# Two feed-forward stages of a macaron block: every pass from the ninth tile on queued in a written order

## The chip, the cores and the metric

The kernel runs on one core of one Trainium2 chip, in one launch. The metric is the device time of an execution in microseconds (us): the median of several runs. The engines are TensorE (PE: matmuls and transposes; its weight loads are shown as PEld), VectorE (DVE), ScalarE (ACT), GpSimd (POOL) and SyncE (SP), which issues DMAs.

## The reference

The input x has the shape (2, 2048, 256) in float32, that is 32 tiles of 128 rows. With `ln` the layer norm without weights:

```
x = x + 0.5 * ffn(ln(x))
x = x + attention(ln(x))
x = x + 0.5 * ffn(ln(x))            # the same weights

ffn(x):   h = silu(q4(x) @ q4(w_gate).T) * (q4(x) @ q4(w_up).T)      # 256 -> 704
          return q4(h) @ q4(w_down).T                                # 704 -> 256
q4(x):    blocks of 16 along the last dimension: scale = max(|x|) / 6, at least 1e-12;
          x / scale rounded to 0, 0.5, 1, 1.5, 2, 3, 4, 6 with its sign; times scale
attention: q, k, v complex (256 -> 512 each, with biases);
          scores = (qr kr^T + qi ki^T) / 16, softmax over 2048 keys; out = [wr, wi] @ Wo.T + bo
```

## The kernel before

x stays on chip for the whole execution, in four groups `xs[g]` of eight tiles (GT = 8, NT = 32). The quantised weights are `wgu` (gate and up) and `wd` (down). The kernel has three stages.

**A feed-forward stage** (`ffn`, once with phase 0 and once with phase 1) does this for each tile. Statistics of a group of eight tiles (`Norm`) come from DVE, with one Sqrt on ACT. ACT normalises four tiles into `xl` (L234), and `quant` rounds them: DVE finds the blocks' maxima (L164), scales (L166), takes reciprocals (L168), multiplies (L170), ACT takes absolute values (L179), two DVE passes round (L180, L182), and the last multiplication goes to POOL (L184). TensorE transposes (tx, L403), ACT copies. `product` multiplies by the gate weights and then by the up weights (gu, L428) into one of two PSUM buffers; ACT takes the silu of the first (L442), DVE multiplies by the second (L446). Two tiles' `h` are rounded together with the same `quant`; `turn` transposes h on TensorE (th, L463) and ACT copies (hqT, L464); `back` multiplies by `wd` (po, L472) and DVE adds the result to x (L474).

**The opening** does this for the first eight tiles beside the preparation of the weights. Its work is cut into generators, called threads, that yield after each pass, and `ORDER` lists which thread takes its next step:

```
for name in ORDER.split():
    next(threads[name])
...
fence(begun)
```

`fence` ties each instruction behind the one before it on its engine, so each engine's queue has the order of the list. From the ninth tile on there is no list: the loop over `units` traces the products of a tile, the last projection of an earlier one and the turn of another, and rounds two tiles at a time (one at a time for the last two). The compiler's scheduler sets the order within the engines' queues by its own priorities. While the first stage runs, the loop around it also calls `batches[0].measure` and `batches[0].turned` (statistics, transposes txa and a product `own` for the first batch's attention), and the first attention steps.

**The attention** runs in steps of 1/8 of a group of four query tiles: eight groups, eight steps each, and ten more at the end. A step makes scores (ps, L708) and keeps the running maximum on DVE (`most`, L720); after the eighth, `peak` transposes it (pm, L727) and DVE forms `mx` (L729 to L732), which `highest` turns back (pb, L737). Later steps subtract and take exponentials (L743, L744), sum the weights on POOL (`sums`, L772) and multiply by the values (m, L805). `plain` makes the values' side of one pair of tiles (xn). `residual` adds the constant row `bout`, the bias with what the value bias gives, to four tiles of x on POOL (L848):

```
nc.gpsimd.tensor_tensor(gr.xo, gr.xo, bout.unsqueeze(1).to_broadcast([P, QG, D]), ALU.add)
```

It is traced in the fifth step after the group's scores, but has no tie to anything except readers of x. Phase 1 of `ffn` starts in the last attention steps.

Of the kernel before, what the change touches and what calls it, by code (L numbers as in the profile page):

```python
# [17 lines left out]
P = 128  # L18
BLK = 16
EPS = 1e-5  # L20

# [9 lines left out]

ORDER = """
# [20 lines left out]
def kernel(ctx: ExitStack, tc: tile.TileContext, x, wqT, bq, wkT, bk, wvT, bv, woT, bo,  # L53
# [84 lines left out]
    ones = const.tile([P, P], FP, tag="ones", name="ones")  # L138
    nc.gpsimd.memset(ones, 1.0)
    tiny = const.tile([P, 1], FP, tag="tiny", name="tiny")  # L140
    nc.gpsimd.memset(tiny, 1e-12)
# [15 lines left out]

    def quant(pool, y, n, tag, last, first=None):
# [7 lines left out]
        nc.vector.scalar_tensor_tensor(scale, scale, 1.0 / 6.0, tiny.to_broadcast([P, nb]), ALU.mult, ALU.max)  # L166
        rec = pool.tile([P, nb], FP, tag=f"{tag}_r", name=f"{tag}_r", bufs=2)
        nc.vector.reciprocal(rec, scale)  # L168
        if first is None:
            nc.vector.scalar_tensor_tensor(  # L170
                yb, yb, BELOW, rec.unsqueeze(2).to_broadcast([P, nb, BLK]), ALU.mult, ALU.mult
            )
        else:
            nc.vector.scalar_tensor_tensor(rec, rec, BELOW, ones[:, 0:nb], ALU.mult, ALU.mult)
            first.tensor_tensor(yb, yb, rec.unsqueeze(2).to_broadcast([P, nb, BLK]), ALU.mult)
# [10 lines left out]
    class Norm:  # L186
# [6 lines left out]
        def turns(self, pool):  # L193
# [4 lines left out]

            mv, bn = tile("mv", [P, n, 2]), tile("bn", [P, n, 6])
# [5 lines left out]
            var = tile("var", [P, n])  # L205
            nc.vector.tensor_scalar(var, mv[:, :, 1], EPS, None, ALU.add)
            yield
# [16 lines left out]
            nc.vector.scalar_tensor_tensor(self.shift, mv[:, :, 0], -1.0, rstd, ALU.mult, ALU.mult)  # L224
# [22 lines left out]
    class Rounding:  # L247
# [9 lines left out]
        def turns(self, y, n):  # L257
# [9 lines left out]
            nc.vector.scalar_tensor_tensor(scale, scale, 1.0 / 6.0, tiny.to_broadcast([P, nb]), ALU.mult, ALU.max)  # L267
# [50 lines left out]
    def fold():  # L318
# [63 lines left out]
        nc.gpsimd.tensor_tensor(bb, bq_sb, bk_sb, ALU.mult)  # L382
        ps = weight_bank([P, KE], "wbb")
# [5 lines left out]
    def ffn(phase, store, pools):  # L389
# [19 lines left out]
        def inputs(i0):  # L409
# [10 lines left out]
            yield  # L420
# [28 lines left out]
        def held(i0, n):  # L449
            h = later["pool"].tile([P, n, FF], FP, tag="h", name=f"h{phase}_{i0}", bufs=3 if phase else 4)  # L450
            for u in range(n):
                hs[i0 + u] = h[:, u, :]
            return h.rearrange("p u i -> p (u i)")

        def turn(i):

            hq = hs.pop(i)
            hqTs[i] = later["pool"].tile([P, NR, P], FP, tag="hqT", name=f"hqT{phase}_{i}", bufs=2)
            for r0 in (0, 4):
# [4 lines left out]
                nc.scalar.copy(hqTs[i][:, r0:r0 + len(rs), :], ps[:, 0:len(rs), :])  # L464
                yield

        def back(i):
            g, j = divmod(i, GT)
            hqT = hqTs.pop(i)
            po = p_acc.tile([P, D], FP, tag="acc", name=f"po{phase}_{i}")  # L470
            for r in range(NR):
                nc.tensor.matmul(out=po, lhsT=hqT[:, r, :], rhs=wd[:, r, :], start=(r == 0), stop=(r == NR - 1))  # L472
# [8 lines left out]
        xqTs, hs, hqTs = {}, {}, {}  # L481
        pending, turned = [], []
        first = 0
        if phase == 0:
            first, pending, stats[1] = opening(across, products, held, turn, back)
            yield
        else:
            for i0 in (0, XT):
                for _ in inputs(i0):
                    yield  # L490
            yield

        units = [(i0, HT) for i0 in range(first, NT - HT, HT)] + [(i0, 1) for i0 in range(NT - HT, NT)]
        for i0, n in units:
            if i0 % XT == 0 and i0 + XT < NT and i0 + XT not in xqTs:
                all_of(inputs(i0 + XT))
            h = held(i0, n)
            for u in range(n):
# [3 lines left out]
                if len(pending) > HT:  # L502
                    all_of(turn(pending[0]))
                    turned.append(pending.pop(0))
                yield
            all_of(quant(later["pool"], h, n * FF, "qh", nc.gpsimd if n == HT else nc.vector))
            pending += range(i0, i0 + n)
        while turned:
            following = pending[:1]
            if following:  # L510
                all_of(turn(pending.pop(0)))
            all_of(back(turned.pop()))
            turned += following
            yield

    def opening(across, products, held, turn, back):
# [41 lines left out]
        return 8, list(range(TURNED, 8)), norms["n2"]  # L558
# [39 lines left out]
    class Batch:  # L598
# [3 lines left out]
        def __init__(self, b):  # L602
            self.b = b
            self.xT, self.xn, self.stats = {}, {}, {}

        def measure(self, part):
            g = self.b * tiles // GT + part
            self.stats[g] = normalise(asmall, g, 0, GT)
# [5 lines left out]
        def turned(self, p, kt):  # L614

            if p == 0 and self.b == 0:
                self.rc = asmall.tile([P, tiles], FP, tag="rc", name=f"rc{self.b}")
            nat = kt.tile([P, 2, D], FP, tag="nat", name=f"nat{self.b}_{p}", bufs=2)
            for v in range(2):
                self.norm(nat[:, v, :], 2 * p + v)  # L620
            ps = p_t.tile([P, KD, 2, P], FP, tag="t", name=f"txa{self.b}_{p}")
            for v in range(2):
                for kc in range(KD):
                    nc.tensor.transpose(ps[:, kc, v, :], nat[:, v, ts(kc, P)], ident)  # L624
            self.xT[p] = kt.tile([P, KD, 2, P], FP, tag="xT", name=f"xT{self.b}_{p}", bufs=NP)
            nc.scalar.copy(
                self.xT[p].rearrange("p c v t -> p (c v t)"), ps.rearrange("p c v t -> p (c v t)")
            )
            if self.b == 0:
                for v in range(2):  # L630
                    self.own(nat[:, v, :], 2 * p + v)

# [27 lines left out]
    def attention(batches, at, kt, late):  # L660
# [80 lines left out]
        def weights(gr, s):  # L741
# [5 lines left out]
            if not seven(gr):  # L747
# [3 lines left out]
                else:  # L751
                    for v in range(2):
                        add(gr.sums, gr.sums, both[:, v, :, :], ALU.add)
# [4 lines left out]
        def sums_of_weights(gr, s):  # L758
# [12 lines left out]
            else:  # L771
                add(gr.sums, t[:, 1:3, :], gr.first[:, 1:3, :] if s == 1 else gr.sums, ALU.add)  # L772
# [72 lines left out]
        def residual(gr):  # L845
            g, j = divmod(gr.i * QG, GT)
            gr.xo = xs[g][:, j:j + QG, :]
            nc.gpsimd.tensor_tensor(gr.xo, gr.xo, bout.unsqueeze(1).to_broadcast([P, QG, D]), ALU.add)  # L848
# [160 lines left out]
```

## Time and profile before

| what | us |
|---|---|
| median of 3 runs (lowest to highest) | 1071.6 (1071.26 to 1072.62) |
| the profiled execution | 1072.21 |
| its span, first to last instruction | 1070.4 |
| busy: TensorE matmuls, weight loads | 1047.0, 733.0 |
| busy: DVE, ACT, POOL | 805.9, 470.0, 255.9 |

The mean granted clock of TensorE was 0.998. A line of the profile's groups names the line of the kernel, the engine, the operation and what it writes and reads. A matrix instruction's busy time overlaps that of the next one. In float32 each product of the program appears as two matmul instructions, each transpose as one.

### The profile page before, as it was taken

How to read it: one execution, taken by the hardware profiler on the slowest of the kernel's cores; microseconds unless marked ns; L12 is line 12 of the kernel's file. 1: busy time of each engine (PE TensorE's matmuls, PEld its weight loads, DVE VectorE, ACT ScalarE, POOL GpSimd, SP SyncE). 2: the span in 40 equal slices, each digit the busy share in tenths (PEclk: the TensorE clock that was granted, in tenths of full speed). 3: DMA queues.
4: the chain of work that ended last, by engine and by line, in shares of the span. 5: the costliest groups of instructions: out<-in, count | busy, mean ns of one | idle time of the engine just before them, and what ended most of it. 6: DMA issues, size and time to landing. Idle time of an engine off the chain costs nothing.

```text
span 1070.4 us, 11326 instructions
## 1 busy us (share of the span) xinstructions
PE 1047.0 (98%) x4206; PEld 733.0 (68%) x4206; DVE 805.9 (75%) x1387; ACT 470.0 (44%) x739; POOL 255.9 (24%) x148
## 2 busy tenths in 40 slices
PE   6998999999999999999999999999999999999998
PEld 5676777777765567676675767666655777777776
DVE  7999998867634888576698958678777577777575
ACT  4744644544235635446444533343343244343232
POOL 4564121210103020111124111212481021221110
PEclk9999999999999999999999999999999999999999
DMA  9000000000000000000000000000000000000001
GB/s 320 2 1 1 1 1 1 1 1 1 0 1 1 1 0 1 1 1 1 0 1 1 1 0 1 1 1 1 0 1 1 10 20 10 20 12 19 20 10 40
DMA packets 7286, 13.50 MB, mean 13 GB/s; under 512 B 1344, under 2 KB 3648, under 8 KB 6848
## 3 DMA queue, kind: packets, MB, share of 16 engines
q1 hardware_dynamic: 6128, 12.13, 3.1%
q10 hardware_dynamic: 1104, 0.66, 0.3%
q8 instruction: 33, 0.54, 0.2%
q14 instruction: 21, 0.17, 0.0%
HBM read 8.59 MB, written 4.19 MB: 12 GB/s over the span
## 4 chain that ended last, share of the span: by engine, by line
PE 91%; DVE 5%; ACT 2%; DMA 1%; issue 0%; POOL 0%; ACTq 0%; DVEq 0%; POOLq 0%
PE gu L428 26%; PE ps L708 19%; PE m L805 15%; PE po L472 14%; PE th L463 4%; PE poa L856 3%; PE z L783 3%; PE pu L686 2%; PE tx L403 1%; PE wm L338 1%; PE txa L624 1%; ACT xn L234 1%; DVE h L285 1%; DMA n_gate<-in_w_gate_dram 1%; DVE h L283 1%
## 5 line engine op out<-in xcount | busy, mean ns | idle before, releaser
L428 PE MATMUL gu<-wgu,xqT 128*128 128x352 f32 x1024 | 319.1, 461 | 3.0 <-DVE h L446 2.7
L428 PEld LDWEIGHTS gu<-wgu,xqT 128*128 128x128 f32 x1024 | 188.9, 191 | 98.2 <-DVE h L446 3.8
L708 PE MATMUL ps<-uT,xT 128*128 128x512 f32 x512 | 232.2, 593 | 0.7 <-DVE most L720 0.7
L472 PE MATMUL po<-wd,hqT 128*128 128x256 f32 x768 | 176.1, 379 | 0.0
L472 PEld LDWEIGHTS po<-wd,hqT 128*128 128x128 f32 x768 | 144.7, 190 | 28.2 <-ACT zT L819 0.6
L708 PEld LDWEIGHTS ps<-uT,xT 128*128 128x128 f32 x512 | 95.1, 190 | 93.2 <-issue 81.0
L720 DVE TENSOR_TENSOR most<-ps,most 128x512 f32<-128x512 f32 x112 | 77.0, 687 | 93.5 <-ACT st L715 92.9
L184 POOL TENSOR_TENSOR h<-h,qh_s 128x1408 f32<-128x1408 f32 x26 | 67.5, 2594 | 290.1 <-DVE h L182 248.2
L715 ACT COPY st<-ps 128x512 f32<-128x512 f32 x128 | 74.5, 583 | 134.1 <-PE ps L708 133.6
L805 PE MATMUL m<-tw,xn 128*128 128x256 f32 x448 | 124.9, 380 | 0.0
L464 ACT COPY hqT<-th 128x512 f32<-128x512 f32 (+1 forms) x128 | 55.5, 481 | 156.7 <-PE th L463 154.5
L772 POOL TENSOR_TENSOR sums<-tw,sums 128x512 f32<-128x512 f32 x42 | 56.9, 1354 | 232.2 <-DVE tw L768 212.9
L805 PE MATMUL m<-st,xn 128*128 128x256 f32 x336 | 100.0, 379 | 0.0
L744 ACT ACTIVATE st<-st 128x1024 f32<-128x1024 f32 x64 | 67.4, 1057 | 72.7 <-DVE st L743 72.0
L446 DVE TENSOR_TENSOR h<-h,gu 128x704 f32<-128x704 f32 x64 | 56.3, 879 | 53.3 <-PE gu L428 50.6
L805 PEld LDWEIGHTS m<-tw,xn 128*128 128x128 f32 x448 | 84.8, 190 | 13.1 <-DVE tw L767 1.2
L743 DVE TENSOR_TENSOR st<-st,top 128x1024 f32<-128x1024 f32 x64 | 82.8, 1305 | 0.8 <-ACT top L739 0.8
L805 PEld LDWEIGHTS m<-st,xn 128*128 128x128 f32 x336 | 63.2, 190 | 26.2 <-issue 19.4
L180 DVE SCALAR_TENSOR_TENSOR h<-qh_m,h 128x1408 f32<-128x1408 f32 (+1 forms) x30 | 45.8, 1527 | 33.1 <-ACT qh_m L179 32.9
L442 ACT ACTIVATE h<-gu 128x704 f32<-128x704 f32 x64 | 48.2, 753 | 44.7 <-PE gu L428 44.6
L179 ACT ACTIVATE qh_m<-h 128x1408 f32<-128x1408 f32 (+1 forms) x30 | 38.9, 1297 | 46.1 <-DVE h L170 42.3
L463 PE MATMUL th<-ident,h 128*128 128x128 f32 x384 | 53.1, 273 | 1.4 <-ACT hqT L464 1.4
(175 smaller groups left out, 1266.6 us busy)
## 6 DMA issues: line engine op xcount, KB each, us to landing
out_dram<-x SPq DMA_DIRECT2D x15, 256.0 KB, 2.1
x<-in_x_dram SPq DMA_DIRECT2D x3, 1024.0 KB, 13.0
n_down<-in_w_down_dram SPq DMA_DIRECT2D x1, 704.0 KB, 9.4
n_up<-in_w_up_dram SPq DMA_DIRECT2D x1, 640.0 KB, 6.0
x<-in_x_dram ACTq DMA_DIRECT2D x1, 512.0 KB, 5.3
wq_sb<-in_wqT_dram SPq DMA_DIRECT2D x1, 512.0 KB, 7.0
wk_sb<-in_wkT_dram SPq DMA_DIRECT2D x1, 512.0 KB, 4.7
wv_sb<-in_wvT_dram SPq DMA_DIRECT2D x1, 512.0 KB, 6.6
```

Source lines behind the costliest of these rows:

```text
L184: last.tensor_tensor(yb, yb, scale.unsqueeze(2).to_broadcast([P, nb, BLK]), ALU.mult)
L428: nc.tensor.matmul(out=ps[:, b2, 0:HALF], lhsT=xqT[:, i % XT, kc, :], rhs=wgu[:, kc, ts(which * 2 + b2, HALF)], start=(kc == 0), stop=(kc ...
L446: nc.vector.tensor_tensor(h, h, up, ALU.mult)
L463: nc.tensor.transpose(ps[:, r - r0, :], hq[:, chunk(r)], ident)
L472: nc.tensor.matmul(out=po, lhsT=hqT[:, r, :], rhs=wd[:, r, :], start=(r == 0), stop=(r == NR - 1))
L708: scored = nc.tensor.matmul(out=ps, lhsT=gr.of.xT[s][:, c, v, :], rhs=gr.uT[:, c, :], start=(c == 0), stop=(c == KD - 1),)
L715: nc.scalar.copy(piece[:, v, :], ps)
L720: seen = nc.vector.tensor_tensor(gr.most, ps, gr.most, ALU.max)
L743: nc.vector.tensor_tensor(piece, piece, gr.top.unsqueeze(1).to_broadcast([P, 2, Q]), ALU.subtract)
L744: nc.scalar.activation(piece, piece, AF.Exp, scale=SCALE)
L772: add(gr.sums, t[:, 1:3, :], gr.first[:, 1:3, :] if s == 1 else gr.sums, ALU.add)
L805: i = nc.tensor.matmul(out=gr.m[k], lhsT=left, rhs=right, start=first, stop=last)
```

## The change

- **Both feed-forward stages from the ninth tile on are threads.** `woven` makes a thread for every group's statistics (`n`), four input tiles (`x`), pair of `h` to be rounded (`h`), tile's products (`p`), turn (`t`) and last projection (`b`); in the first stage also the attention's statistics (`m`), batch 0's transposes (`a`) and its first six steps (`q`). `FFN0_ORDER` (492 steps) and `FFN1_ORDER` (422) list which one goes on, and `fence` ties each engine's queue to that order. A new generator `rounding` yields after each pass. The second stage keeps the loop for its first eight tiles, with the input tiles traced earlier.
- **All transposes of this part are TensorE's**; `turn` writes into a pool of its own with three buffers (`hqT2`).
- **The last two tiles of the second stage go in halves** of 352 columns (`halves`), each with products, silu, multiplication and rounding on DVE.
- **The bias** is queued on POOL behind the group's latest sum of weights. The values' side of batch 1 (`plain`) leaves one step out after half of its pairs.
- The lower bound of the scales and two factors become immediate constants in place of constant tensors (`tiny`, `ones`); `Norm` forms the negative mean (`least`) earlier.

```diff
+FFN0_ORDER = """
+t4 n2 n2 x12 t5 x12 n2 p9 n2 p8 m0 p9 x12 n2 p8 t4 n2 x12 n2 n2 x12 p9 n2 n2 n3 p8 x12 x12 b4 p8 x12
+n2 t6 p9 h8 h8 n3 t5 x12 x12 x12 p11 p11 h8 p10 x12 n2 n3 n2 p11 p10 t6 p11 n3 n2 h8 n2 x12 h8 p10
...
+p31 b25 p30 b25 h28 a7 h28 t26 a7 q a7 p31 t26 h28 h28 q a7 b24 t27 h30 b24 q h30 h30 b26 t29 b26
+h30 h30 b27 t28 t29 b27 h30 h30 q a5 h30 b29 a5 b29 a5 t28 b28 t30 b28 t31 a5 q t30 a7 t31 b31 b30
+b31 a5 a7 b30
+"""
+FFN1_ORDER = """
+h6 n3 n2 h6 b3 p8 h6 p8 n3 h6 p8 p9 n2 n2 n2 h6 p8 n2 n2 p9 t4 p9 h6 t4 h6 t5 p10 t5 p9 n2 p11 n2
+p10 h8 n2 h8 h8 n2 p10 h6 n2 t6 n2 n2 p11 n3 n2 n2 n2 h8 t6 n3 b3 x16 x16 b4 h8 x16 t7 p10 h8 x16 b4
...
+p28 h28 h26 t25 h28 t25 h30a b23 t26 h28 t26 h28 h30a h30b b23 b24 h28 h30b h28 h30a t27 h30b h31b
+h30a b25 t27 h30a b24 h28 b26 h30b h28 h31a h30a h30a h31b b26 t29 h30b h30a h30b h31b b25 h31a h31b
+h31b h30b t28 h30b h30b h31b b27 t29 h31b h31a h31b t28 b27 t30 h31a h31a b28 h31a b28 h31b h31a
+h31a t30 h31a b29 b29 t31 t31 b30 b30 b31 b31
+"""
...
+    def rounding(pool, tag, y):
+        n = y.shape[1]
...
         yb = y.rearrange("p (b k) -> p b k", k=BLK)
         scale = pool.tile([P, nb], FP, tag=f"{tag}_s", name=f"{tag}_s", bufs=2)
         nc.vector.tensor_reduce(scale, yb, AX.X, ALU.max, apply_absolute_value=True)
         yield
-        nc.vector.scalar_tensor_tensor(scale, scale, 1.0 / 6.0, tiny.to_broadcast([P, nb]), ALU.mult, ALU.max)
+        nc.vector.tensor_scalar(scale, scale, 1.0 / 6.0, TINY, ALU.mult, ALU.max)
+        yield
         rec = pool.tile([P, nb], FP, tag=f"{tag}_r", name=f"{tag}_r", bufs=2)
+        nc.vector.reciprocal(rec, scale)
+        yield
+        nc.vector.scalar_tensor_tensor(
+            yb, yb, BELOW, rec.unsqueeze(2).to_broadcast([P, nb, BLK]), ALU.mult, ALU.mult
+        )
+        yield
+        m = pool.tile([P, n], FP, tag=f"{tag}_m", name=f"{tag}_m", bufs=1)
+        nc.scalar.activation(m, y, AF.Abs, scale=STEPS)
+        yield
+        nc.vector.scalar_tensor_tensor(y, m, LEAST, y, ALU.max, ALU.add)
+        yield
+        nc.vector.scalar_tensor_tensor(y, m, LEAST, y, ALU.max, ALU.subtract, reverse1=True)
+        yield
+        nc.gpsimd.tensor_tensor(yb, yb, scale.unsqueeze(2).to_broadcast([P, nb, BLK]), ALU.mult)
+        yield
...
+        rec = pool.tile([P, nb], FP, tag=f"{tag}_r", name=f"{tag}_r", bufs=2)
+        nc.vector.tensor_scalar(scale, scale, 1.0 / 6.0, TINY, ALU.mult, ALU.max)
...
-            nc.vector.scalar_tensor_tensor(rec, rec, BELOW, ones[:, 0:nb], ALU.mult, ALU.mult)
+            nc.vector.tensor_scalar(rec, rec, BELOW, None, ALU.mult)
...
         def held(i0, n):
-            h = later["pool"].tile([P, n, FF], FP, tag="h", name=f"h{phase}_{i0}", bufs=3 if phase else 4)
+            pool, bufs = (later["pool"], 4 - phase) if phase or i0 else (wpool, 1)
+            h = pool.tile([P, n, FF], FP, tag="h", name=f"h{phase}_{i0}", bufs=bufs)
             for u in range(n):
                 hs[i0 + u] = h[:, u, :]
-            return h.rearrange("p u i -> p (u i)")
+            wholes[i0] = h.rearrange("p u i -> p (u i)")
+            return wholes[i0]

         def turn(i):

+            if i in hqTs:
+                return
             hq = hs.pop(i)
-            hqTs[i] = later["pool"].tile([P, NR, P], FP, tag="hqT", name=f"hqT{phase}_{i}", bufs=2)
+            pool, tag = place()
+            hqTs[i] = [(r, wd[:, r, :]) for r in range(NR)], pool.tile([P, NR, P], FP, tag=tag, name=f"hqT{phase}_{i}", bufs=3 if tag == "hqT2" else 2)
+            hqT = hqTs[i][1]
             for r0 in (0, 4):
                 ps = p_t.tile([P, 4, P], FP, tag="t", name=f"th{phase}_{i}_{r0}")
                 rs = range(r0, min(r0 + 4, NR))
                 for r in rs:
                     nc.tensor.transpose(ps[:, r - r0, :], hq[:, chunk(r)], ident)
-                nc.scalar.copy(hqTs[i][:, r0:r0 + len(rs), :], ps[:, 0:len(rs), :])
+                nc.scalar.copy(hqT[:, r0:r0 + len(rs), :], ps[:, 0:len(rs), :])
                 yield
+        def place():
+            if "turned" in later:
+                return later["turned"], "hqT2"
+            return (later["pool"] if phase else wpool), "hqT"

...
-            hqT = hqTs.pop(i)
+            chunks, hqT = hqTs.pop(i)
             po = p_acc.tile([P, D], FP, tag="acc", name=f"po{phase}_{i}")
-            for r in range(NR):
-                nc.tensor.matmul(out=po, lhsT=hqT[:, r, :], rhs=wd[:, r, :], start=(r == 0), stop=(r == NR - 1))
+            for k, (r, right) in enumerate(chunks):
...
-        xqTs, hs, hqTs = {}, {}, {}
+        def woven(order, pending, more):
+            begun = len(nc.cur_bb.bb.instructions)
+            single = NT - HT if store else NT
+            def tile_products(i):
+                if i not in hs:
+                    held(i - i % HT, HT)
+                yield from products(i)
+            def inputs_of(i0):
+                g, j0 = divmod(i0, GT)
+                xl = xp.tile([P, XT, D], FP, tag="xl", name=f"xl{phase}_{i0}")
+                for u in range(XT):
+                    normed(xl[:, u, :], g, j0 + u, stats[g])
+                    yield
+                yield from rounding(xp, "qx", xl.rearrange("p u d -> p (u d)"))
+                for u in range(0, XT, 2):
+                    across(i0, xl[:, u:u + 2, :], u, 2)
+                    yield
+            def pair_of(i0):
+                yield from rounding(later["pool"], "qh", wholes[i0])
+            def halves(i, b2):
+                if i not in hs:
+                    held(i, 1)
+                h = hs[i][:, ts(b2, HALF)]
+                gu = []
+                for which in range(2):
+                    gu.append(p_big.tile([P, 2, 512], FP, tag="big", name=f"gu{phase}_{i}_{b2}{which}")[:, 0, 0:HALF])
+                    for kc in range(KD):
+                        nc.tensor.matmul(
+                            out=gu[which],
+                            lhsT=xqTs[i - i % XT][:, i % XT, kc, :],
+                            rhs=wgu[:, kc, ts(which * 2 + b2, HALF)],
+                            start=(kc == 0),
+                            stop=(kc == KD - 1),
+                        )
+                    yield
+                    if which == 0:
+                        nc.scalar.activation(h, gu[0], AF.Silu)
+                        yield
+                nc.vector.tensor_tensor(h, h, gu[1], ALU.mult)
+                yield
+                yield from quant(later["pool"], h, HALF, "qh", nc.vector)
+                yield
+            threads = dict(more)
+            for i0 in range(GT + XT * (1 + phase), NT, XT):
+                threads[f"x{i0}"] = inputs_of(i0)
+            for g in range(2, NG):
+                stats[g] = Norm(g, 0, GT)
+                threads[f"n{g}"] = stats[g].turns(small)
+            for i0 in sorted(i for i in hs if i not in pending and i % HT == 0) + list(range(GT, single, HT)):
+                threads[f"h{i0}"] = pair_of(i0)
+            for i in range(single, NT):
+                for b2 in range(2):
+                    threads[f"h{i}" + "ab"[b2]] = halves(i, b2)
+            for i in range(pending[0], NT):
+                threads[f"t{i}"] = turn(i)
+            for i in range(GT, single):
+                threads[f"p{i}"] = tile_products(i)
+            for i in range(pending[0], NT):
+                threads[f"b{i}"] = back(i)
+            for name in order.split():
+                next(threads[name])
+            for name, thread in threads.items():
+                assert next(thread, None) is None and next(thread, threads) is threads, name
+            fence(begun)
...
+        xqTs, hs, hqTs, wholes = {}, {}, {}, {}
+        if phase == 0:
+            pending, stats[1] = opening(across, products, held, turn, back)
+            yield
+            woven(FFN0_ORDER, pending, later["more"])
+            return
...
+        for i0 in range(0, GT, HT):
+            h = held(i0, HT)
+            coming = inputs(i0 + XT + HT) if i0 % XT == XT - HT else None
...
+                if coming and u == 0:
+                    while next(coming) != "rounded":
+                        pass
+                elif coming:
+                    all_of(coming)
                 yield
-            all_of(quant(later["pool"], h, n * FF, "qh", nc.gpsimd if n == HT else nc.vector))
-            pending += range(i0, i0 + n)
-        while turned:
-            following = pending[:1]
-            if following:
-                all_of(turn(pending.pop(0)))
-            all_of(back(turned.pop()))
-            turned += following
-            yield
+            if i0 + HT < GT:
+                all_of(quant(later["pool"], h, HT * FF, "qh", nc.gpsimd))
+                pending += range(i0, i0 + HT)
+        woven(FFN1_ORDER, pending, {f"b{i}": back(i) for i in turned})
...
         def measure(self, part):
             g = self.b * tiles // GT + part
-            self.stats[g] = normalise(asmall, g, 0, GT)
+            self.stats[g] = Norm(g, 0, GT)
+            return self.stats[g].turns(asmall)
...
             else:
-                add(gr.sums, t[:, 1:3, :], gr.first[:, 1:3, :] if s == 1 else gr.sums, ALU.add)
+                gr.summed = add(gr.sums, t[:, 1:3, :], gr.first[:, 1:3, :] if s == 1 else gr.sums, ALU.add)
                 gr.first = None
...
         def residual(gr):
             g, j = divmod(gr.i * QG, GT)
             gr.xo = xs[g][:, j:j + QG, :]
-            nc.gpsimd.tensor_tensor(gr.xo, gr.xo, bout.unsqueeze(1).to_broadcast([P, QG, D]), ALU.add)
+            with tc.issue_after(gr.summed.ins):
+                nc.gpsimd.tensor_tensor(gr.xo, gr.xo, bout.unsqueeze(1).to_broadcast([P, QG, D]), ALU.add)
...
+    ffn0_pools[1]["turned"] = ffn0.enter_context(tc.tile_pool(name="f0_t", bufs=1, side="right"))
...
-    begun = 0
-    done = 0
-    for n, _ in enumerate(stage, GT - 2):
-        if n >= tiles + 4 and begun < NP:
-            if begun % (GT // 2) == 0:
-                batches[0].measure(begun // (GT // 2))
-            batches[0].turned(begun, kt)
-            begun += 1
-        if n >= NT - 2:
+    done = 6
+    def scored():
+        for _ in range(done):
             next(att)
-            done += 1
+            yield
+    more = {f"m{part}": batches[0].measure(part) for part in range(tiles // GT)}
+    more.update({f"a{p}": batches[0].turned(p, kt) for p in range(NP)})
+    more["q"] = scored()
+    ffn0_pools[1]["more"] = more
+    all_of(stage)
     ffn0.close()
-    late["pool"] = ctx.enter_context(tc.tile_pool(name="late", bufs=1, side="right"))
+    late_stack = ctx.enter_context(ExitStack())
+    late["pool"] = late_stack.enter_context(tc.tile_pool(name="late", bufs=1, side="right"))
     per = tiles // QG * NP
-    plain = [(done + p, 0, p) for p in range(NP)] + [(per + LAG + p + 1, 1, p) for p in range(NP)]
+    plain = [(done + p, 0, p) for p in range(NP)] + [(per + LAG + p + 1 + (p >= NP // 2), 1, p) for p in range(NP)]
...
-    for _ in stage:
-        pass
+    late_stack.close()
+    hp["turned"] = ctx.enter_context(tc.tile_pool(name="f1_t", bufs=1, side="right"))
+    all_of(stage)
```

## The prediction

> **What bounds the kernel now.** I read the page's busy shares and slices first, then the waits of TensorE, then the stretches around the change, then single instructions in the timeline.
>
> ```profile
> PE 1047.0 (98%) x4206; PEld 733.0 (68%) x4206; DVE 805.9 (75%) x1387; ACT 470.0 (44%) x739; POOL 255.9 (24%) x148
> ...
> PE   6998999999999999999999999999999999999998
> ...
> DVE  7999998867634888576698958678777577777575
> ```
>
> TensorE is busy all the time, so nothing shortens the kernel except less matmul work or fewer gaps on TensorE. DVE is nearly full in the slices up to about 215 us and has room later.
>
> "Busy" overstates TensorE, since its instructions overlap; what counts is the distance from start to start:
>
> ```profile
> 89.38 7.26 PE L428 MATMUL gu<-wgu,xqT 128*128 128x352 f32 x24
> ```
>
> 24 of them take 7.26 us with the last one's 0.46, so 6.80 / 23 = 0.2955 us each, though one lasts 0.46. In the same way, from other rows of the timeline: 0.2155 us for 256 columns, 0.109 for a transpose, 0.429 for 512 columns.
>
> The replaced first stretch runs from tile 8's first product (89.1 us) to the end of the sixth attention step (339.6). It holds 384 gate and up matmuls (113.5 us), 336 of the last projection (72.4), 240 transposes (168 th, 40 tx, 32 txa: 26.2), 48 score matmuls (20.6) and 32 of the queries (6.9): 239.6 us of work in 250.5 us. So 10.9 us are gaps or a slow clock. Where:
>
> ```profile
> 89.10:98.60 9.50, 7.54 (x27) 4.59 (x25) 9.47 (x15) 2.74 (x5) 2.59 (x1) 1.00 0.00 1
> 98.60:104.50 5.90, 5.26 (x17) 3.14 (x18) 5.73 (x19) 0.83 (x2) 1.93 (x1) 0.71 0.00 0
> 104.50:126.70 22.20, 20.41 (x94) 15.31 (x92) 21.25 (x46) 14.02 (x23) 4.52 (x2) 1.00 0.00 1
> 126.70:215.00 88.30, 87.59 (x380) 64.58 (x381) 79.42 (x127) 44.72 (x69) 18.87 (x8) 1.00 0.00 1
> 89.10:339.60 250.50, 244.69 (x1043) 175.64 (x1041) 187.98 (x302) 115.69 (x193) 47.94 (x20) 0.99 0.00 1
> ...
> 580.00:588.00 8.00, 5.70 (x22) 3.01 (x21) 7.79 (x14) 2.27 (x4) 3.85 (x3) 1.00 0.00 0
> ...
> 850.00:1067.00 217.00, 216.40 (x959) 162.69 (x957) 155.63 (x181) 79.69 (x129) 38.81 (x16) 1.00 0.05 18
> ```
>
> (Columns: stretch, length, busy us of PE, PEld, DVE, ACT and POOL, granted clock, DMA.) Where PE has gaps, DVE has none: 9.47 of 9.50, 5.73 of 5.90. After the first gap the clock was 0.71 over 5.9 us, which costs 0.29 x 5.9 = 1.7 us. The waits of TensorE from 89 to 340 us name the two causes:
>
> ```profile
> PE gu L428 <- DVE h L446: 2.7, 2, 2.0
> PE tx L403 <- POOL xl L184: 2.4, 2, 1.8
> ```
>
> A product waits until DVE has emptied a PSUM bank; transposes wait for a rounded input. In both, DVE was doing something less urgent.
>
> **The change part by part.** *TensorE's work:* turns, products, last projections and the six `q` steps are the same matmuls, and transposes were on TensorE already. So 0 us, and what can be won is gaps alone.
>
> *First stage in one given order.* I summed the passes that FFN0_ORDER lists, with durations of this trace (DVE: pair passes of 128x1408 1.61 each, reciprocal 0.69, scale 0.25, multiplication 0.88, addition 0.415; input passes of 128x1024 1.22; statistics 0.41; POOL 2.61 and 1.94). The whole order holds 239.5 us of TensorE, 196 of DVE, 120 of ACT and 41 of POOL. Running sums: when TensorE has 75.6 us behind it, DVE has 70.8; at 150.8, 139.7; at the end DVE is 43 behind. So DVE fills 94% of the first 75 us and 76% of the rest. Next I took the TensorE work ahead of each consumer, minus the DVE work (and POOL pass) ahead of its producer. All are positive if DVE never waits; the narrowest are p11's bank (3.0 us), x12's transposes (3.7), p15's bank (3.9), t15 (4.9); from x24 on all exceed 8. DVE enters late: its last pass of the opening ends at 92.8, TensorE starts tile 8 at about 89.2, so 3.6 us. That makes p11 wait some 0.6 us, and the others have little left for ACT's part of a rounding.
>
> How much is left as gaps? Lower end: 0.6. Upper end: the opening, the one part that already runs in a given order, lost 2.6 us between 27 and 89 us with DVE at 98%, or 4.2%; over 250 us that is 10.5. The new order resembles it only in its first 75 us: 4.2% of 75 = 3.2. I add 0.5 for the rest and 0.9 for half a chance of one more slow-clock stretch of 1.7. I take 4.6 us, against 10.9 now: **saved 6.3**.
>
> [...] Here a gap of 2.04 us was followed by 0.71, while one of 1.85 us at 126.75 was followed by 1.00. [...]
>
> *Statistics, batch 0's transposes and query steps* are now threads: each `a` still issues two ACT passes, four transposes, a copy and two DVE products; each `n` or `m` one Sqrt with its table loads (1.28 us each). They are in the sums above. ACT has half of its time free, which hides them; a silu behind a Sqrt could be some 2.8 us late, inside the leads except in the first 75 us.
>
> *Bias added later.* Before, the eight POOL additions of 128x1024 went wherever their readers were done, four at 331 to 342 us, one at the worst place:
>
> ```profile
> 334.43 2.33 DVE L697 TENSOR_SCALAR rcg<-rc,bqbk 128x4 f32<-128x4 f32 x1
> ...
> 584.82 2.39 POOL L848 TENSOR_TENSOR x<-x,bout 128x1024 f32<-128x1024 f32 x1
> ...
> 585.64 1.58 DVE L731 TENSOR_TENSOR mx<-mx,rcg 128x4 f32<-128x4 f32 x1
> ...
> 587.57 0.62 PE L737 MATMUL pb<-ident,mx 128*128 128x128 f32 x4 [1.58 <-DVE mx L732]
> ```
>
> A four-element DVE pass, 0.15 to 0.22 us otherwise, took 1.58 and 2.33 beside POOL's 2.4 us, and TensorE waited. Gaps around these: 1.2 us at 339 to 344, and 0.89 + 1.75 = 2.6 at 581.9 and 587.6. Now each addition is queued on POOL behind a sum of weights in step 4 of its group; the maximum's chain runs in step 7 and later, some 20 us away. Behind it on POOL stand the next group's or steps' sums, whose readers (the freeing of `tw`, then the values) have a step of about 7 us. Additions at 555.6, 572.0 and 599.3 delayed no matmul, so moved ones cost 0, or 2.4 if that cover fails. The `plain` of batch 1 also skips step 39, whose DVE was full (7.79 of 8.00). Saved between 0 and 3.8; I take 0.8 + 2.0 = **2.8**, since other passes remain there.
>
> *Second stage.* From 850 us there is 214.6 us of matmul work in 217.0 with the last one's end, about 2 us of gaps. DVE enters with no arrears; sums in its order: 49.9 of DVE at 56.4 of TensorE, 167.6 at 210.3. Narrowest leads 2.6 and 3.3 us, from x24 on over 14. Best 0.7 left, worst 4.2% of 217 = 9.1. I take 1.5: **saved 0.5**.
>
> *Tiles 30 and 31 in halves.* A DVE pass of 128x704 is 0.89, of 128x1408 1.62, so each cut adds 0.16; twelve cut passes (1.9 us) and four times half a scale and reciprocal more (1.3) add some 3 us of DVE, where it has 35 us of lead. The last store follows the last addition as before: 0. *Scale without a constant tensor, the new `least`, a third `hqT`:* below 0.1 us each on DVE, hidden by the same leads; 0 in the first stage too, where one more 0.16 pass would cost at most itself.
>
> [...] Beside POOL, DVE passes of two SBUF tensors got longer (128x128: 1.32 instead of 0.28). The order has 17 POOL passes in the first stage. From its DVE work between each and the next two-tensor pass I get an estimate of 11 us blocked in all, 3.5 of it in the first 75 us. [...]
>
> [...]
>
> **Sum.** 6.3 + 2.8 + 0.5 = 9.6 us. From the profiled execution's 1072.2 (span 1070.4): 1062.6. The median of the runs, 1071.6, is 0.6 lower, so 1062.0.
>
> **The rivals.** [...]
>
> *B. Fixed orders stall at the head of queues, slower:* in a strict order nothing can pass a late pass, and TensorE stalls at the opening's 4.2% everywhere. The first stage then keeps 10.5 us (saves 0.4), the second has 9.1 (costs 7.1), attention still saves 2.8: 1071.6 + 3.9 = 1075.5. It decides once the second stage has over 5.2 us of gaps (2 now) while the first saves only 0.4. For it: only 2 us can be won from 850 us on, 7 lost. Against: leads above 13 us there.
>
> *C. Evened out:* the first stage has 7 us of gaps (saves 3.9), the second 6 (costs 4.0), and attention saves nothing: 1071.7.
>
> *D. The bias does not move* where TensorE waits, or something else fills its place: 2.8 missing: 1064.8.
>
> **How the numbers follow.** The measurement tells about 0.2%, 2.1 us, from no change. Forecast 0.46, A 0.14, D 0.08: together faster, 0.68. C: 0.08. B: 0.24. Lowest bound: all gaps but 0.6 and 0.7 gone and 3.8 in attention, 10.3 + 3.8 + 1.3 = 15.4, 1056.2. The range leaves out that extreme and B's end: 1057.0 to 1074.5; the forecast with A and D alone would be 1057 to 1067.
>
> **What would show it.** Right: the first stage with its six score steps ends near 333 us instead of 339.6; the two waits above fall under 1 us each; no x<-x,bout at 331 to 342 or 585; DVE's share in the first 75 us above 95%. Wrong: new waits of gu on h or tx on xl after 180 us, th on hqT, a clock below 1.00 after 110 us, or more than 4 us of gaps from 850 us on.

## The result and the profile after

The changed kernel takes 1058.5 us, the kernel before 1071.8 beside it: a ratio of 0.9875 (95% interval 0.9858 to 0.9892), or 13.4 us less. The forecast was 1062.0 (1057.0 to 1074.5). The profiled execution took 1058.3 with a span of 1056.5.

The same parts of the page of the changed kernel:

```profile
PE 1040.6 (98%) x4206; PEld 732.0 (69%) x4206; DVE 808.1 (76%) x1408; ACT 470.0 (44%) x742; POOL 259.3 (25%) x148
...
PE   6999999999999999999999999999999999999998
...
DVE  7998998896764987566778967676868569878875
```

TensorE has the same 4206 matmuls and the same 98%; DVE is 2 us busier. Nothing here shows a gain, since the engines did nearly the same work in a shorter span. The stretches that begin at the ninth tile show it. They are cut at the places of the earlier table, and the columns are the same (length, busy us of PE, PEld, DVE, ACT, POOL, clock, DMA):

```profile
89.20:98.70 9.50, 9.50 (x38) 6.28 (x36) 8.44 (x27) 6.31 (x11) 2.59 (x1) 1.00 0.00 1
98.70:104.60 5.90, 5.90 (x29) 4.59 (x28) 5.41 (x9) 2.19 (x4) 0.00 (x0) 1.00 0.00 0
104.60:126.80 22.20, 22.20 (x101) 16.74 (x100) 21.04 (x31) 9.48 (x15) 4.52 (x2) 1.00 0.00 1
...
89.20:329.30 240.10, 239.86 (x1037) 175.05 (x1035) 187.84 (x298) 110.79 (x179) 43.39 (x18) 1.00 0.00 1
```

TensorE is busy 9.50 of 9.50, 5.90 of 5.90, 22.20 of 22.20, at full clock, and DVE has a little idle time where it had none. The first stage with its six score steps now needs 240 us for 239.6 us of matmuls. All waits of TensorE between 89 and 850 us (total, times, longest):

```profile
PE tx L471 <- ACT hqT L538: 0.6, 1, 0.6
PE po L552 <- DVE most L876: 0.2, 1, 0.2
```

None is left after 850 us. For the account I summed, over each stretch, the distances from one matmul's start to the next less the usual distance of its size (gaps and slow clock together):

| stretch (ended by) | before | after |
|---|---|---|
| first matmul's start, and the opening | 8.3 + 8.9 | 8.0 + 8.5 |
| first stage from tile 8 to the 48th score matmul | 10.4 | 1.2 |
| attention, to its last score matmul | 5.4 | 2.3 |
| rest of attention, second stage's tiles 0 to 7 | 0.4 | 1.3 |
| second stage from tile 8 | 2.1 | 0.4 |

The rows differ by 13.8 us in all, the spans by 13.9. Some 0.7 lies before the changed part and varies from run to run: its first product starts at 89.48 us in this profile and at 90.12 when the changed kernel ran again (`changed_again`). One row got worse.

### The profile page after: what moved, and what is told of

The parts are those of the page before. It is cut to its first block, busy times and chain, and to the rows that moved or that the text cites. A ratio compares the mean times of both kernels' runs of the same rounds, so it can differ in the third digit from the quotient of the medians.

```text
span 1056.5 us, 11296 instructions
## 1 busy us (share of the span) xinstructions
PE 1040.6 (98%) x4206; PEld 732.0 (69%) x4206; DVE 808.1 (76%) x1408; ACT 470.0 (44%) x742; POOL 259.3 (25%) x148
## 4 chain that ended last, share of the span: by engine, by line
PE 93%; DVE 4%; DMA 1%; ACT 0%; issue 0%; SPq 0%; DVEq 0%; ACTq 0%
PE gu L496 27%; PE ps L864 20%; PE po L552 16%; PE m L961 15%; PE th L537 4%; PE poa L1013 3%; PE z L939 3%; PE pu L842 3%; PE tx L471 1%; PE gu L595 1%; DMA wq_sb<-in_wqT_dram 1%; PE txa L777 1%; DMA n_up<-in_w_up_dram 1%; DVE bn L267 0%; PE pm L883 0%
## 5 line engine op out<-in xcount | busy, mean ns | idle before, releaser
L496 PE MATMUL gu<-wgu,xqT 128*128 128x352 f32 x992 | 307.5, 460 | 0.9 <-DVE sd L281 0.5
L496 PEld LDWEIGHTS gu<-wgu,xqT 128*128 128x128 f32 x992 | 183.5, 190 | 92.8 <-issue 2.6
L220 POOL TENSOR_TENSOR h<-h,qh_s 128x1408 f32<-128x1408 f32 x24 | 63.6, 2649 | 265.4 <-DVE h L218 237.6
L538 ACT COPY hqT<-th 128x512 f32<-128x512 f32 (+1 forms) x128 | 58.4, 479 | 155.6 <-PE th L537 152.9
L961 PEld LDWEIGHTS m<-tw,xn 128*128 128x128 f32 x448 | 84.8, 190 | 13.4 <-DVE tw L923 1.0
L537 PEld LDWEIGHTS th<-ident,h 128*128 128x128 f32 x384 | 47.3, 141 | 17.4 <-issue 8.0
L537 PE MATMUL th<-ident,h 128*128 128x128 f32 x384 | 57.0, 273 | 0.3 <-ACT hqT L538 0.3
L216 DVE SCALAR_TENSOR_TENSOR h<-qh_m,h 128x1408 f32<-128x1408 f32 x24 | 41.5, 1731 | 19.1 <-ACT qh_m L213 19.0
```

What stands on the lines that cost most here:

```text
L220: nc.gpsimd.tensor_tensor(yb, yb, scale.unsqueeze(2).to_broadcast([P, nb, BLK]), ALU.mult)
L496: nc.tensor.matmul(out=ps[:, b2, 0:HALF], lhsT=xqT[:, i % XT, kc, :], rhs=wgu[:, kc, ts(which * 2 + b2, HALF)], start=(kc == 0), stop=(kc ...
L537: nc.tensor.transpose(ps[:, r - r0, :], hq[:, chunk(r)], ident)
L538: nc.scalar.copy(hqT[:, r0:r0 + len(rs), :], ps[:, 0:len(rs), :])
L961: i = nc.tensor.matmul(out=gr.m[k], lhsT=left, rhs=right, start=first, stop=last)
```

## The experiments

Each kernel below was timed beside the kernel before, which had medians of 1071.6 to 1072.0 on those chips. The changed kernel itself took 1058.5 us the first time and 1058.9 the second, so half a microsecond between two medians shows little; where less than 1 us is at stake, the gaps in the traces decide.

**One stage at a time.** `first_alone` leaves `woven` to phase 0; phase 1 runs by the old loop:

```diff
+        units = [(i0, HT) for i0 in range(first, NT - HT, HT)] + [(i0, 1) for i0 in range(NT - HT, NT)]
+        for i0, n in units:
...
-        woven(FFN1_ORDER, pending, {f"b{i}": back(i) for i in turned})
...
```

> The changed kernel, but the second stage runs by the old loop over units (tiles of the second stage not in a written order, last tiles whole); first stage in its order, bias tied, batch 1's values shifted. Theory (gaps are filled where each part is, and the parts add): the second stage's 2 us of gaps come back, so 1058.5 + 2 = 1060.5 us, with TensorE's gaps before 830 us as in the changed kernel. Rival (the second stage's order won more than its own gaps, for instance by letting attention's end overlap): 1063 or more.

Measured: 1059.2 us. The second stage's gaps came back (2.1 us from its tile 8 on, 0.7 of them its old wait of `th`), but 0.9 us of gaps ahead of it went. So the second stage's part of the change is worth 0.8 us, by the medians and by these gaps alike, less than its own gaps.

`second_alone` does the reverse, with `woven(FFN0_ORDER, ...)` replaced by the old loop and the old calls around it.

> The changed kernel, but the first stage from the ninth tile on runs by the old loop; the second stage's order, the tied bias and batch 1's shift stay. Theory: the first stage's gaps, some 10 us, come back: 1058.5 + 10 = 1068.5 us, with waits of gu on h and of tx on xl near 99, 103 and 127 us and a clock below 1 after the first. Rival (the first stage's gain came from the tie of the bias at 331 to 342 us): about 1062.

Measured: 1067.6 us, so the first stage's order is worth 9.1 us. The waits came back at their places. TensorE from 89 to 850 us in this run, and the stretch with the slow clock:

```profile
PE gu L496 <- DVE h L514: 2.8, 2, 2.0
PE tx L471 <- POOL xl L249: 2.2, 2, 1.7
```

```profile
98.60:104.50 5.90, 5.34 (x18) 3.11 (x18) 5.74 (x18) 0.82 (x3) 1.93 (x1) 0.71 0.00 0
```

The bias is tied in this kernel, so the rival, that the tie won the first stage's time, falls. The third `hqT`, the immediate constants and the new `Norm` are in this kernel too, and its row for the first stage is 10.1 us, against 10.4 in the kernel before; so these smaller edits win at most 0.3 us there.

**What in the order does it.** `no_tie` traces the same lists but drops one line:

```diff
             for name, thread in threads.items():
                 assert next(thread, None) is None and next(thread, threads) is threads, name
-            fence(begun)
```

> The changed kernel with both written orders kept as the order in which the program is traced, but without the fence, so that nothing ties an instruction to the one before it on its engine and the compiler's scheduler may reorder. Theory (the fixed order in each queue is what fills the gaps): several us of gaps come back in the two stages, 1062 to 1068 us. Rival (tracing the passes in this sequence is enough, the scheduler keeps nearly this order): within 1 us of 1058.5.

Measured: 1067.2 us; 8.7 us of the 13.4 are gone. The sequence in the program is not enough; the ties hold each queue to it. (Whether another written order, tied, would do as well was not tried.) From 89 us to the end TensorE's three longest waits were for other things than in the old loop:

```profile
PE po L552 <- ACT hqT L538: 2.9, 1, 2.9
PE gu L496 <- ACT h L510: 1.6, 1, 1.6
PE th L537 <- ACT xT L779: 1.3, 1, 1.3
```

All three ended with ACT. At 99.27 us a product waited for a silu that stood behind the loading of a table (1.28 us) after a Sqrt.

**How close the first stage runs.** `late_3us` and `late_10us` put 8 and 24 needless DVE passes ahead of the order:

```diff
 FFN0_ORDER = """
+z z z z z z z z 
 t4 n2 n2 x12 t5 x12 n2 p9 n2 p8 m0 p9 x12 n2 p8 t4 n2 x12 n2 n2 x12 p9 n2 n2 n3 p8 x12 x12 b4 p8 x12
...
+            def extra():
+                bn = small.tile([P, 6], FP, tag="zz", name=f"zz{phase}", bufs=1)
+                for _ in range(8):
+                    nc.vector.bn_stats(bn, xs[0][:, 0, :])
+                    yield
...
```

> The changed kernel with eight needless statistics passes (0.41 us each, 3.3 us of DVE in all) ahead of all DVE passes of the first stage's order. In the changed kernel the input x12 is ready 0.7 us before its transposes and p9's bank is free 0.2 us before p11 needs it. Theory (DVE has no slack in the first 15 us of the order, and TensorE takes the delay over less these margins): gaps of 2.5 to 3.2 us in TensorE near 102 to 113 us, 1061 to 1061.5 us, more by up to 1.7 if the clock falls. Rival (DVE's 43 us of slack over the stage absorbs it): within 0.7 us of 1058.5.

> The same with 24 needless passes, 9.8 us of DVE. Theory: TensorE loses 9 to 9.7 us in the first 25 us of the order and nothing later, and the clock falls to half once or twice (1.7 us each): 1067.5 to 1071.5. Rival (slack absorbs most): under 1063.

Measured: 1059.5 and 1068.1 us. The passes held DVE longer than expected: each starts 0.46 us after the one before it, so the first statistics behind them begin 3.6 and 11.0 us late. TensorE waited once in each run. The waits of the one and then of the other:

```profile
PE tx L472 <- POOL xl L221: 1.2, 1, 1.2
```

```profile
PE gu L497 <- DVE h L515: 7.1, 1, 7.1
```

In start-to-start distances these are 1.3 and 7.3 us, so some 2.2 and 3.7 us were absorbed. Both expectations fail: TensorE did not take the whole delay, and 43 us of slack did not swallow it. Part of it went into DVE's own waits for ACT and TensorE, which are gone in both runs (0.96 us at 95.0 and 0.35 at 99.0 in the changed kernel). The rest is the margin of the consumer that came late first. That is x12's transposes in the one run, with the 0.7 us of the expectation. In the other it is p11's first product, and the expectation has its margin wrong. In `late_3us` this product starts while p9's multiplication has not begun:

```profile
102.32 7.27 PE L497 MATMUL gu<-wgu,xqT 128*128 128x352 f32 x24
...
103.33 0.83 DVE L515 TENSOR_TENSOR h<-h,gu 128x704 f32<-128x704 f32 x1
```

So it needs only the multiplication before that one, p8's, which in the changed kernel ended at 100.26 us for a start at 102.42: 2.2 us to spare, not 0.2. Nothing later in the order was late in either run. The second run lost about 2.4 us more to a halved clock (0.80 on average from 101 to 118 us). So the order starts with 2 to 4 us to spare on DVE, by consumer; beyond that nearly the whole delay reaches TensorE.

**The bias.** `bias_alone` puts two edits into the kernel before:

```diff
...
-            nc.gpsimd.tensor_tensor(gr.xo, gr.xo, bout.unsqueeze(1).to_broadcast([P, QG, D]), ALU.add)
+            with tc.issue_after(gr.summed.ins):
+                nc.gpsimd.tensor_tensor(gr.xo, gr.xo, bout.unsqueeze(1).to_broadcast([P, QG, D]), ALU.add)
...
-    plain = [(done + p, 0, p) for p in range(NP)] + [(per + LAG + p + 1, 1, p) for p in range(NP)]
+    plain = [(done + p, 0, p) for p in range(NP)] + [(per + LAG + p + 1 + (p >= NP // 2), 1, p) for p in range(NP)]
```

> The kernel before with two edits alone: the bias queued behind the sum of weights, and batch 1's values one step later from its fifth pair on. Theory (POOL's addition holds up DVE's small passes before TensorE's wait): the gaps of 1.2 us at 339 to 344 and 2.6 us at 582 to 588 go, 1071.8 - 3 = 1069 us. Rival (something else becomes late in the same place): 1071 to 1072.

Measured: 1068.3 us, 3.5 us faster. The additions moved to 381, 437, 498, 560 us and so on (in the changed kernel they start between 371.6 and 774.0, none near 331 to 342 or 585). The waits of `pb` and `pm` are gone and no others came in their place, so that rival falls.

`both_free` takes the same two edits out of the changed kernel, `plain_old` only the shift of `plain`, `bias_free` only the tie.

> The changed kernel with the bias not tied to the sums and batch 1's values at their old steps. Theory: the attention's two places lose again what they lost before, 1.2 + 2.6 us, less where the first stage's order has moved the steps: 1058.5 + 3 = 1061.5. Rival (with the attention's first steps moved into the first stage, the bias finds harmless places by itself): within 0.5 us of 1058.5.

> The changed kernel with the values' side of batch 1 at its old steps; the bias stays queued behind the sums. The kernel without either lost 10.2 us: 7.4 of gaps at 341 to 345 and 348.7 with a halved clock, 2.6 at 579 and 585. Theory (POOL's bias addition is what blocks DVE, the shift adds little): at most 1 us lost, 1058.5 to 1059.5. Rival (step 39 is too full for DVE even without the bias): the 2.6 us at 570 to 575 come back, 1061.

> The changed kernel with only the tie of the bias taken away; batch 1's shift stays. The kernel with neither took 1068.7, and the shift alone taken away cost 0.2. Theory (the tie carries both places): 1068 to 1069, with additions at 331 to 348 us and TensorE waiting for mx and most beside them, and at 580 to 588 again. Rival (the shift alone would have mended the place at 579 to 585): 1066, with the first place's gaps only.

Measured: 1068.7, 1058.7 and 1068.4 us; the changed kernel took 1058.9 when it ran beside `bias_free`. So the shift is worth at most 0.2 us, and the tie 9.5 us here, against 3.5 for both in the old kernel. My expectation for `both_free` (1061.5) was wrong by 7 us: the parts do not add. POOL's, DVE's and TensorE's rows of `bias_free` show why (start, us, engine, line, what):

```profile
335.26 4.91 POOL L1004 TENSOR_TENSOR x<-x,bout 128x1024 f32<-128x1024 f32 x2 [0.57 <-ACT xn L300]
```

```profile
335.32 2.45 DVE L811 TENSOR_TENSOR xn<-xn 128x128 f32<-128x128 f32 x1
...
337.90 2.42 DVE L813 TENSOR_TENSOR xn<-xn 128x128 f32<-128x128 f32 x1
...
341.31 3.32 PE L864 MATMUL ps<-uT,xT 128*128 128x512 f32 x4 [3.86 <-DVE most L876]
...
348.52 0.62 PE L893 MATMUL pb<-ident,mx 128*128 128x128 f32 x4 [1.39 <-DVE mx L888]
```

Two additions in a row hold POOL for 4.91 us. Two small DVE passes of about 0.28 us take 2.45 and 2.42 beside them. The running maximum stands behind those, and the next scores wait 3.86 us for their PSUM bank. In the old kernel the sixth score step ended at 339.6 us, so these passes of `plain`, which follow it, began at 341, when the additions (331 to 342) were nearly over:

```profile
339.93 2.35 POOL L848 TENSOR_TENSOR x<-x,bout 128x1024 f32<-128x1024 f32 x1 [0.67 <-ACT xn L234]
```

```profile
340.96 1.47 DVE L655 TENSOR_TENSOR xn<-xn 128x128 f32<-128x128 f32 x1
...
342.36 0.28 DVE L656 TENSOR_TENSOR xn<-xn 128x128 f32<-128x128 f32 x1
```

The new order has six steps done by 324 us, `plain` comes 6 us earlier, and it meets the additions, which did not move. Of the 9.7 us of gaps that the attention has more than in the changed kernel, 7.5 lie here and 2.3 at the second place (579 to 585 us). And the gap costs clock:

```profile
335.00:355.00 20.00, 14.75 (x39) 7.02 (x38) 15.02 (x22) 10.91 (x19) 7.17 (x3) 0.91 0.00 0
```

A clock of 0.91 over 20 us is 1.8 us more. The same stretch of the changed kernel has TensorE busy 19.97 of 20.00 and POOL idle:

```profile
335.00:355.00 20.00, 19.97 (x68) 11.69 (x69) 15.86 (x49) 13.92 (x23) 0.00 (x0) 1.00 0.00 0
```

**Halves.** `whole_tiles` gives the steps of the first halves to whole tiles:

```diff
+            def whole(i, b2):
+                if b2 == 1:
+                    for _ in range(9):
+                        yield
+                    return
...
+                yield from products(i)
+                yield from quant(later["pool"], hs[i], FF, "qh", nc.vector)
+                yield
...
-                    threads[f"h{i}" + "ab"[b2]] = halves(i, b2)
+                    threads[f"h{i}" + "ab"[b2]] = whole(i, b2)
```

> The changed kernel with tiles 30 and 31 of the second stage as wholes: the products, silu, multiplication and rounding of a tile all stand where the first half's steps stand in the order. Theory (DVE leads by over 30 us there, so the halves bring nothing): within 0.3 us of the changed kernel. Rival (halves shorten the end): 0.5 to 1 us slower, with a gap in TensorE before the last turns.

Measured: 1060.2 us, the changed kernel beside it 1058.9: 1.3 us slower, the rival and somewhat more. TensorE waits before one of the last turns:

```profile
1047.97 0.89 DVE L249 TENSOR_TENSOR h<-h,qh_s 128x704 f32<-128x704 f32 x1
...
1049.01 0.85 PE L537 MATMUL th<-ident,h 128*128 128x128 f32 x6 [1.34 <-DVE h L249]
```

Neither the kernel before nor `first_alone`, whose old loops round the same two tiles whole, has this wait. So it belongs to whole tiles at these places of this order; an order rewritten for whole tiles was not tried. From tile 8 of the second stage on, `whole_tiles` has 1.9 us of gaps, the old loop 2.1 and the changed kernel 0.4: nearly all that the second stage's order won, it won with the halves.

**A version meant to be faster.** The worse row of the account is a gap of 0.77 us at 837.8, where the transposes of x12 follow the six of a turn directly. `tx_earlier` moves them ahead of the last projection:

```diff
                 all_of(products(i0 + u))
+                if coming and u == 1:
+                    all_of(coming)
                 if turned:
                     all_of(back(turned.pop()))
...
-                elif coming:
-                    all_of(coming)
                 yield
```

> The changed kernel with the transposes of x8 and x12 in the second stage's first eight tiles moved ahead of the same step's last projection and turn. In the changed kernel TensorE waits 0.77 us at 837.8, where these transposes stand right behind six others and both PSUM buffers still wait for ACT's copies. Theory: that gap goes and nothing takes its place, since 2.6 us of projection now lies between the two groups of transposes: 0.8 us less than the changed kernel on the same chip, about 1057.7. Rival (the copies are then late for the turn behind): no change within 0.2.

> The changed kernel once more, beside its variants on the same chip: 1058.5, as before, with 0.3 either way.

Measured: 1058.0 us (1057.8 to 1058.7, four runs) and 1058.9 (1058.6 to 1059.0). The medians differ as I expected, but the trace does not bear it out. The gap only moved to the next user of those PSUM banks, 0.68 us instead of 0.77:

```profile
838.39 3.72 PE L1013 MATMUL poa<-wvo,zT 128*128 128x256 f32 x16 [0.51 <-ACT hqT L538]
```

From tile 8 of the first stage on, the two profiled runs' gaps differ by 0.1 us; the rest of the 0.9 lies in the first 90 us, which the edit does not touch. So the rival holds: the next step behind the turn waits instead. That this version is faster is not shown.

## Why the prediction was right, and where its sizes were off

**TensorE bound by gaps alone** held: the same work, start to start, to the us, and every lost us found as a gap or a slow clock.

**First stage: 6.3 us expected, 9.2 in the account, 9.1 by `second_alone`.** This is the term that was mis-sized. I left 4.6 us of gaps in it, of which 3.2 came from carrying the opening's 4.2% into the first 75 us; 1.2 were left in the whole stage. The opening's row fitted the load of DVE but not the case. My reading, which no run tests, is that passes in the opening have no such leads. The leads I had counted came out, if anything, too short. I had p11's bank 0.6 us late and x12's transposes just in time; measured, p8's multiplication had been over for 2.2 us when p11's product started, and x12 was ready at 109.02 for transposes at 109.74:

```profile
99.37 0.89 DVE L514 TENSOR_TENSOR h<-h,gu 128x704 f32<-128x704 f32 x1 [0.35 <-PE gu L496]
```

```profile
102.42 7.27 PE L496 MATMUL gu<-wgu,xqT 128*128 128x352 f32 x24
...
109.74 0.60 PE L471 MATMUL tx<-ident,xl 128*128 128x128 f32 x4
```

```profile
107.09 1.93 POOL L220 TENSOR_TENSOR xl<-xl,qx_s 128x1024 f32<-128x1024 f32 x1 [12.95 <-DVE xl L218]
```

Nothing was late, so no gap came, and without a gap there was no slow clock either (0.9 in my sum). DVE's share in that time was 69.9 of 75.6 us, 92.5%, where I had named over 95% as a sign:

```profile
89.20:164.80 75.60, 75.60 (x324) 54.94 (x322) 69.92 (x127) 40.05 (x61) 16.16 (x7) 1.00 0.00 1
```

The stage with its six score steps ended at about 329 us, not 333.

**Bias: 2.8 us expected, 3.5 by `bias_alone`, 3.1 in the account.** Right in mechanism and nearly in size for the kernel before: the first place gave 0.75 us where I had 0.8, the second 2.6 where I had 2.0. One line of it was misread. DVE had nothing to do for 2.14 us after the pass of 2.33 at 334.43, so that pass delayed no matmul; in `bias_alone` it takes 0.22, and DVE's next pass follows 4.46 us after its start in both. What counted at the first place was the `xn` pass of 1.47 at 340.96. I also had the shift of `plain` helping at the second place; `plain_old` shows that the shift alone is worth 0.2 at most once the bias is tied. And I treated the terms as independent. Without the tie the new order would have lost 9.5 us again, so some 70% of the change's gain hang on one edit that looked like the smaller part. Nothing in the prediction saw this; that the tie stood in the same change was luck for the forecast.

**Second stage: 0.5 us expected, 0.8 measured** (1.7 won from its tile 8 on, most of it with the halves, and 0.9 lost just ahead of it).

**Halves: 0 expected, 1.3 measured.** Here a step failed. I read DVE's lead of 35 us off two running sums. But the last tiles' passes on DVE need products that TensorE makes only shortly before (in `whole_tiles` DVE sat idle for 2.23 us at 1041.7 until the last product was done), so DVE cannot use that lead there. What counts is the chain: in `whole_tiles` it takes 6.3 us from the end of the last multiplication (1042.60) to the end of the rounding (1048.86), through seven DVE passes and one of ACT, with too little else for TensorE. In the changed kernel the chain of the last half takes 4.0 us (1042.92 to 1046.90), and no turn waits for it.

**The rivals.** A (DVE late because its passes get longer beside POOL's, 1066.0) was there but not on the path. If I take every DVE pass beside POOL that lasted at least 15% and 0.1 us longer than the middle one of its kind without POOL, the first stage lost 15.8 us in 12 passes, more than the 11 I had estimated, and more than the 10.5 of the old loop; 2.8 us of it fell in the first 75 us, where the old loop lost 5.6. That the later leads of over 8 us took the rest is my reading; TensorE did not wait for any of these passes. B and C did not happen: from tile 8 of the second stage on TensorE waited for nothing. D fell with `bias_alone`.

**The clock.** Idle gaps of 1.16 us (`late_3us`), 1.34 (`whole_tiles`) and 1.85 (before) left the clock at full; gaps of 2.04 us (before), 2.87 (`no_tie`) and 3.86 (`bias_free`) were followed by half a clock for 3.4 us, one of 7.1 us (`late_10us`) by 6.8 us of it. In the clock records of the kernel before and of the changed one, each slow stretch begins a whole number of times 3.413 us after the clock first rose to full: 24 times behind the gap of 2.04 us and 308 at the end in the kernel before, 305 at the end of the changed one. So where a gap falls between such points may count beside its length, and no single length is shown to be the limit.

## What to carry to other kernels

When the bound engine's work is fixed, count it start to start, stretch by stretch, and the remainder is all there is to win; then price a written order by the margin at its first few consumers, not by the average load of the helping engine. A lead from running sums can mislead: near the end of a stage, follow the chain from the last product instead. Test parts in both contexts, alone and taken out of the whole: a small tie that kept one engine's long pass away from another's short ones was worth at most 3.5 us in the old order and 9.5 in the new one.

## What had not been expected of the hardware

A 128x1024 addition on POOL (2.35 us) stretched a four-element DVE pass from 0.16 or 0.22 to as much as 2.3 us and a 128x128 pass from 0.28 to 2.45, so what was left of the POOL pass, not the size of the DVE pass, set the price: a 128x128 pass that began 1.03 us after an addition took 1.47, one that began 0.06 us after it 2.45. And a gap of 2.04 us was followed by half of TensorE's clock for 3.4 us, which made that gap cost nearly twice its length; one of 1.85 us was followed by the full clock.
